# Moving the next sequence's norm and gates to other slots of a gated-delta-rule kernel

## The chip, the cores and the metric

The kernel runs on one core of a Trainium2 chip. The core has five engines that work side by side, each through its own instructions in order: TensorE (PE in the profile; its weight loads are listed apart as PEld), VectorE (DVE), ScalarE (ACT), GpSimd (POOL) and SyncE (SP), which here issues nearly all DMAs. The metric is the device time of one execution in microseconds (us): 2072.44 us is the median of three runs of the kernel before the change, which lie between 2071.39 and 2076.25.

## The reference

The input x holds 4 sequences of 512 tokens with 256 channels, in float32. Cut to what matters:

```python
xn = layernorm(x)                                  # per token
q, k, v, z = split(xn @ W_qkvz.T)                  # 16 q/k heads, 32 v/z heads of 128
b, a       = split(xn @ W_ba.T)                    # two gates per v head
q, k, v = silu(causal depthwise conv of width 4 (q, k, v))
beta = sigmoid(b)
g    = -exp(A_log) * softplus(a + dt_bias)         # log decay per token and head
core = chunked gated delta rule(rmsnorm(q), rmsnorm(k), v, g, beta)
h    = norm_w * rmsnorm(core) * silu(z)
s    = h @ W_out.T
ffn  = (silu(xn @ Wg.T) * (xn @ Wu.T)) @ Wd.T      # weights looked up: lut[idx]
out  = x + s * silu(ffn)
```

The chunked rule inverts, per head and chunk, a unit lower triangular matrix, multiplies values and keys by the inverse, and carries a 128 x 128 state from chunk to chunk. Before any head of a sequence can be worked on, two things of that sequence are needed: its normalised input, transposed to channels by tokens (the tile xnT), and its gates for all 32 heads (the tiles bek, neg, egl, gc and lnb, and the running sums of g as rows in DRAM, g_rows and eg_rows).

## The kernel before, in words

**Items and slots.** The unit of work is an item: one q/k head of one sequence, with its two v heads. There are 64 items, 16 for each of the 4 sequences; item n belongs to sequence n // 16. An item's work is cut into some 115 named steps (`STEPS`), and the string `SLOT` (L973 to L982) writes down one slot: the order of the steps, each with a lag. In slot n the step with lag 5 is done for item n - 5. So about 13 items are in flight, one slot does one item's worth of work on every engine, and the 64 items take 77 slots. The loop at L1024 writes out the program slot by slot; L1061 to L1068 then pin that order on each engine, so no engine takes an instruction ahead of its place.

**Filling.** In the first dozen slots the steps with large lags do not exist yet. The longest path of an item runs through GpSimd: `nt` (DVE, L564), then `nd` and `nl` (two trips through DRAM, DMAs on SP), `L0` to `L3` (GpSimd, 62 small operations, L633 and L639), `yd` and `iu` (two more trips), `tp` (DVE, L660), `m1` and `m2` (small matmuls, L672 to L705), and on to the chunk steps.

**Preparing the next sequence.** `normed(b)` and `gated(b)` (L186 to L287) are generators that compute xnT and the gates of sequence b; `both` (L1010) chains them. They stop at each `yield`, and what lies between two stops is called a step here. For a sequence after the first these are:

- s1 load x (four DMAs on SP); s2 statistics of two of the four token blocks (DVE, L195 and L196); s3 of the other two; s4 the two activations for 1/sqrt (ACT, L88); s5 and s6 subtract and scale, two blocks each (DVE, L204); s7 four transposes (PE, L213) and a copy to xnT (ACT, L215); s8 the same for the other half; s9, for sequences 0 and 1 alone, xnT is also written to DRAM;
- g1 sixteen matmuls (PE, L233) and three DVE operations (L242 to L245); g2 two activations; g3 three DVE operations (L250 to L252); g4 four matmuls (PE, L256), three DVE operations (L265 to L267) and three activations; g5 a DVE operation (L273), eight matmuls (PE, L276) and a DVE copy (L281); g6 g_rows to DRAM; g7 an exponential; g8 eg_rows to DRAM.

**Where these steps go.** `SLOT` holds the mark `Y` twice: at its very start, where the next step is `qm` (called first Y here), and in the middle, behind `x1`, `t10` and `cq2`, where the next step is `yk` (second Y). At each mark a counter `due` grows by one, and `prepare` (L1016), called behind every step, lets the generator go on by one step when `due` is above zero and more than one PSUM bank is free. At slot 8 of a sequence (L1028) the generator of the next one is begun. With two marks a slot, s1 goes to the first Y of slot 8, s2 to the second, s3 to the first Y of slot 9, and so on; for the second sequence, which has s9, g1 falls on the second Y of slot 12, and for the third and fourth, without s9, on the first Y of slot 12 of the sequence before (slots 28 and 44 of the program). Counting the banks that the steps of `SLOT` hold, two or more are free at every one of these places, so no step is put off.

**Fillers.** `X` stands four times in `SLOT` and adds a piece of the weight lookups of the feed-forward part to each slot (L298 to L339, DVE). A job of 16 pieces ends every fourth slot, with a DMA out and a few more operations.

**PSUM banks.** The 8 banks are handed out in turn (`Bank`, L69): who takes a bank waits for the last reader of the tile that had it before.

**The start.** Before the first slot DVE zeroes the four `iut` tiles and the two `tpl` tiles (L120, called from L123 and L124), which hold the inverses; the norm of the first sequence follows.

Of the kernel before, what the change touches and what calls it, by code (L numbers as in the profile page):

```python
# [15 lines left out]
B, S, D = 4, 512, 256  # L16
HQK, HV, HD = 16, 32, 128
# [21 lines left out]
def gated_delta_ffn_kernel(  # L39
# [16 lines left out]
    nc = tc.nc  # L56
# [60 lines left out]

    def zeroed(shape, name):
        t = const.tile(shape, F32, tag=name, name=name)
        nc.vector.memset(t, 0.0)  # L120
        return t

    iut = [zeroed([P, NP, NC, P], f"iut{i}") for i in range(NBUF["iut"])]  # L123
    tpl = [zeroed([P, NP, NC, 2 * Q], f"tpl{i}") for i in range(NBUF["tpl"])]  # L124

    lid = const.tile([R * LH, Q // R, Q], F32, tag="lid", name="lid")
# [856 lines left out]
    plan = [(name, int(lag or 0)) for name, _, lag in (key.partition(":") for key in SLOT.split())]  # L983
# [10 lines left out]
    PASSES.update(dict.fromkeys("tk tq tv0 tv1 th0 th1 ks1 ks2 ks3 pv0 pv1 pv2 pv3 ps0 ps1 ps2 po0".split(), 2))  # L994
    spare, needed = 0, None
    traced = nc.cur_bb.bb.instructions
    begin = traced[-1]
    items, kept, slot = [], [], 0

    def item(n):  # L1000
        return items[n] if 0 <= n < total else None

    def feed():

        nonlocal spare, needed
        while needed is not None and spare >= needed and len(free) > 2:
            spare -= needed
            needed = next(feeding, None)

    def both(b):  # L1010
        yield from normed(b)
        yield from gated(b)

    due = 0

    def prepare():  # L1016

        nonlocal due
        if due and len(free) > 1:
            due -= 1  # L1020
            while next(preparing, None):
                pass

    for n in range(total + last_lag):  # L1024
        if n < total:
            items.append(Item(n))
            b, hq = divmod(n, HQK)
            if hq == HQK // 2 and b + 1 < B:  # L1028
                for _ in preparing:
                    pass  # L1030
                due = 0
                preparing = both(b + 1)
        if n == total + 6:
            for _ in looked:
                pass
            needed = next(feeding)
        slot = n
        for name, lag in plan:
            if name == "X":
                if n >= 6:  # L1040
                    next(looked, None)
            elif name == "Y":
                due += 1
            elif name in MERGES:
                if item(n - lag) or item(n - lag - 1):
                    MERGES[name](item(n - lag), item(n - lag - 1))
            elif item(n - lag):
                STEPS[name](item(n - lag))
                due += n < 4 and name[0] in "ac"
                prepare()  # L1050
            elif needed is not None:
                spare += PASSES.get(name, 0)
                feed()
# [54 lines left out]
```

## Time and profile before

| | us |
|---|---|
| median of 3 runs | 2072.44 (2071.39 to 2076.25) |
| the profiled execution, its own time | 2075.89 |
| its span, first to last instruction | 2073.70 |
| PE busy (matmuls) | 1969.2 (95% of the span) |
| DVE busy | 1775.5 (86%) |
| ACT busy | 1621.0 (78%) |
| POOL busy | 1388.5 (67%) |
| one undisturbed slot (23) from its first `ak` matmul to the next slot's | 27.87 |

All sums are made against one profiled execution; 2.19 us of its time lie around the span. Slots can be read from the trace by the `ak` matmuls (L444): step `ak` has lag 1 and stands shortly ahead of the second Y, so the stretch from the `ak` of slot n to that of slot n + 1 holds what was done at the second Y of slot n (some 3 us after its start) and at the first Y of slot n + 1 (some 15 us after it). Where the engines' busy times stand beside such a stretch, the number in parentheses counts instructions. A time in brackets behind a row of the timeline is how long that engine was idle before the instruction, and who ended the idle time.

### The profile page before, as it was taken

How to read it: one execution, taken by the hardware profiler on the slowest of the kernel's cores; microseconds unless marked ns; L12 is line 12 of the kernel's file. 1: busy time of each engine (PE TensorE's matmuls, PEld its weight loads, DVE VectorE, ACT ScalarE, POOL GpSimd, SP SyncE). 2: the span in 40 equal slices, each digit the busy share in tenths (PEclk: the TensorE clock that was granted, in tenths of full speed). 3: DMA queues.
4: the chain of work that ended last, by engine and by line, in shares of the span. 5: the costliest groups of instructions: out<-in, count | busy, mean ns of one | idle time of the engine just before them, and what ended most of it. 6: DMA issues, size and time to landing. Idle time of an engine off the chain costs nothing.

```text
span 2073.7 us, 48691 instructions
## 1 busy us (share of the span) xinstructions
PE 1969.2 (95%) x15744; PEld 1442.6 (70%) x15744; DVE 1775.5 (86%) x4356; ACT 1621.0 (78%) x4689; POOL 1388.5 (67%) x4181
## 2 busy tenths in 40 slices
PE   6468999999999999999999999999999999998999
PEld 3235777777777777777777777777777777775755
DVE  7788999999999999999998999999999988862323
ACT  5467889888888888888888888888888989963321
POOL 0777777777777767777777767777777777780000
PEclk9779999999999999999999999999999999999999
DMA  2343443344433444334443344443344343321211
GB/s 76 98 107 89 123 106 103 96 108 120 116 103 100 105 111 105 104 100 110 123 108 101 91 119 103 112 105 102 97 113 123 104 108 100 100 75 44 71 51 51
DMA packets 371885, 206.40 MB, mean 100 GB/s; under 512 B 224544, under 2 KB 353712, under 8 KB 371632
## 3 DMA queue, kind: packets, MB, share of 16 engines
q1 hardware_dynamic: 371632, 203.29, 37.3%
q8 instruction: 126, 2.06, 0.4%
q14 instruction: 127, 1.04, 0.2%
HBM read 179.05 MB, written 24.13 MB: 98 GB/s over the span
## 4 chain that ended last, share of the span: by engine, by line
PE 73%; DVE 16%; POOL 3%; ACT 3%; DMA 3%; issue 1%; SPq 1%; DVEq 0%; POOLq 0%; ACTq 0%
PE av L444 9%; PE pp L824 8%; PE pz L478 7%; PE pv L746 5%; PE po L781 4%; PE ak L444 4%; PE pgu L907 4%; PE kk L556 4%; PE po L778 3%; PE aq L444 3%; PE ps L759 3%; PE ks L729 3%; PE th L510 2%; PE pW L703 2%; PE ptv L510 2%; DVE v L456 2%
## 5 line engine op out<-in xcount | busy, mean ns | idle before, releaser
L633 POOL TENSOR_TENSOR pr<-nl,yl 128x60 f32<-128x60 f32 (+24 forms) x1984 | 584.0, 294 | 220.7 <-ACT ik L88 47.6
L639 POOL TENSOR_TENSOR yl<-yl,pr 128x60 f32<-128x60 f32 (+24 forms) x1984 | 605.1, 305 | 155.7 <-DMA yd<-yl 0.4
L456 DVE SCALAR_TENSOR_TENSOR v<-av,cw,v 128x509 f32<-128x509 f32 (+2 forms) x384 | 282.4, 735 | 0.6 <-ACT v L450 0.3
L478 PE MATMUL pz<-xnT,wz 128*128 128x512 f32 x512 | 242.4, 596 | 4.4 <-DVE acc L836 2.5
L824 PE MATMUL pp<-wo,zT 128*128 128x256 f32 x1024 | 243.7, 381 | 0.5 <-DVE zT L816 0.2
L444 PE MATMUL av<-xnT,wv 128*128 128x512 f32 x512 | 241.3, 594 | 1.4 <-DMA wv<-in_w_qkvz 1.4
L824 PEld LDWEIGHTS pp<-wo,zT 128*128 128x128 f32 x1024 | 185.0, 190 | 25.2 <-issue 2.9
L599 POOL TENSOR_TENSOR qe<-qe,q 128x384 f32<-128x384 f32 x128 | 126.3, 1008 | 100.6 <-DMA qe<-eg_rows 52.3
L86 ACT ACT_TABLE_LOAD x128 | 164.2, 1283 | 3.1 <-PEq L1098 0.8
L92 ACT ACT_TABLE_LOAD x128 | 164.2, 1283 | 2.3
L88 ACT ACTIVATE ds<-ds,ls 128x128 f32<-128x128 f32 x512 | 156.9, 390 | 8.2 <-DVE ls L532 6.6
L738 DVE SCALAR_TENSOR_TENSOR r<-ks,neg,vt 128x128 f32<-128x128 f32 x384 | 116.0, 343 | 44.7 <-PE ks L729 42.9
L456 DVE SCALAR_TENSOR_TENSOR q<-aq,cw,q 128x509 f32<-128x509 f32 (+2 forms) x192 | 142.3, 741 | 13.1 <-ACT q L450 10.8
L503 ACT ACTIVATE junk_o<-po 128x128 f32<-128x128 f32 x512 | 142.1, 278 | 14.3 <-PE po L781 2.1
L478 PEld LDWEIGHTS pz<-xnT,wz 128*128 128x128 f32 x512 | 95.5, 190 | 78.8 <-issue 61.2
L456 DVE SCALAR_TENSOR_TENSOR k<-ak,cw,k 128x509 f32<-128x509 f32 (+2 forms) x192 | 141.4, 736 | 2.0 <-ACT k L450 1.6
L746 PEld LDWEIGHTS pv<-r,iut 128*128 128x128 f32 x768 | 105.6, 191 | 46.0 <-issue 38.2
L444 PE MATMUL ak<-xnT,wk 128*128 128x512 f32 x256 | 135.1, 653 | 0.5 <-DMA wk<-in_w_qkvz 0.5
L444 PEld LDWEIGHTS av<-xnT,wv 128*128 128x128 f32 x512 | 87.6, 191 | 65.6 <-issue 63.9
L746 PE MATMUL pv<-r,iut 128*128 128x128 f32 x768 | 124.8, 285 | 8.4 <-DVE r L738 7.5
L444 PE MATMUL aq<-xnT,wq 128*128 128x512 f32 x256 | 120.7, 594 | 2.8 <-DMA wq<-in_w_qkvz 1.8
L495 DVE TENSOR_SCALAR ds<-ds,gc 128x128 f32<-128x128 f32 x512 | 120.9, 305 | 2.0
(177 smaller groups left out, 5058.1 us busy)
## 6 DMA issues: line engine op xcount, KB each, us to landing
ds<-g_rows SPq DMA_DIRECT2D x64, 512.0 KB, 4.0
nl<-nd SPq DMA_DIRECT2D x256, 128.0 KB, 3.9
qe<-eg_rows SPq DMA_DIRECT2D x64, 384.0 KB, 4.3
wv<-in_w_qkvz SPq DMA_DIRECT2D x128, 128.0 KB, 2.4
wz<-in_w_qkvz SPq DMA_DIRECT2D x64, 256.0 KB, 2.8
wo<-in_w_out SPq DMA_DIRECT2D x64, 256.0 KB, 3.1
wk<-in_w_qkvz SPq DMA_DIRECT2D x64, 128.0 KB, 2.5
wq<-in_w_qkvz SPq DMA_DIRECT2D x64, 128.0 KB, 2.3
```

Of the source, the lines that this page charges most:

```text
L86: nc.scalar.preload_act_table_set("natural_log_exp_and_others")
L88: nc.scalar.activation(out, in_, func, **kw)
L92: nc.scalar.activation(out, in_, AF.Silu)
L444: nc.tensor.matmul(ps, lhsT=getattr(it, "w" + x)[:, d, :], rhs=it.xnT[:, d, :], start=(d == 0), stop=(d == DC - 1),)
L456: nc.vector.scalar_tensor_tensor(y[:, sh:], ps[:, : S - sh], cw[:, block(it.hq), j : j + 1], y[:, sh:], ALU.mult, ALU.add)
L478: nc.tensor.matmul(ps, lhsT=it.wz[:, d, p * P : (p + 1) * P], rhs=it.xnT[:, d, :], start=(d == 0), stop=(d == DC - 1),)
L503: nc.scalar.activation(junk, ps[:, c, :], AF.Square, accum_out=out[:, c : c + 1])
L599: nc.gpsimd.tensor_tensor(it.qe[:, p], it.qe[:, p], thirds(it.q, NC)[:, 1:, :], ALU.mult)
L633: nc.gpsimd.tensor_tensor(pr[:, :k, :n], nl[:, j : j + 1, j + 1 :].to_broadcast([R * LH, k, n]), yl[:, :k, j : j + 1].to_broadcast([R * LH ...
L639: nc.gpsimd.tensor_tensor(yl[:, :k, j + 1 :], yl[:, :k, j + 1 :], pr[:, :k, :n], ALU.subtract)
L746: nc.tensor.matmul(pv[:, p, :], lhsT=it.iut[:, p * NC + c, :], rhs=it.r[:, p, :] if c else vt[:, c, :], start=True, stop=True,)
L824: nc.tensor.matmul(ps[:, j, :], lhsT=chunk(hT, 2 * c2 + j), rhs=it.wo[:, p, :], start=(p == 0), stop=(p == NP - 1),)
```

## The change

Three things. The zeroing of `iut` and `tpl` goes from VectorE to GpSimd. The preparation of the next sequence begins at slot 5 (in the first sequence) or slot 4 (in the second and third) in place of slot 8. And the marks do not all count any more: in the first sequence both Y count as before; in later ones only the second Y counts in slots 4 to 10 of the sequence, and both in slots 11 to 15 and 0 to 3.

```diff
     def zeroed(shape, name):
         t = const.tile(shape, F32, tag=name, name=name)
-        nc.vector.memset(t, 0.0)
+        nc.gpsimd.memset(t, 0.0)
         return t
@@
+    last_y = max(i for i, (name, _) in enumerate(plan) if name == "Y")
@@
-            if hq == HQK // 2 and b + 1 < B:
+            if hq == (4 if b else 5) and b + 1 < B:
                 for _ in preparing:
                     pass
                 due = 0
@@
-        for name, lag in plan:
+        for name_at, (name, lag) in enumerate(plan):
             if name == "X":
                 if n >= 6:
                     next(looked, None)
             elif name == "Y":
-                due += 1
+
+                due += n < HQK or n % HQK >= 11 or n % HQK < 4 or name_at == last_y
```

From this follow the places of the steps (1 and 2 are the first and second Y of a slot of the program):

| steps | before | after |
|---|---|---|
| second sequence, s1 to s9 | 8.1, 8.2, 9.1, 9.2, 10.1, 10.2, 11.1, 11.2, 12.1 | 5.1, 5.2, 6.1, 6.2, 7.1, 7.2, 8.1, 8.2, 9.1 |
| second sequence, g1 to g8 | 12.2, 13.1, 13.2, 14.1, 14.2, 15.1, 15.2, 16.1 | 9.2, 10.1, 10.2, 11.1, 11.2, 12.1, 12.2, 13.1 |
| third sequence, s1 to s8 | 24.1, 24.2, 25.1, 25.2, 26.1, 26.2, 27.1, 27.2 | 20.2, 21.2, 22.2, 23.2, 24.2, 25.2, 26.2, 27.1 |
| third sequence, g1 to g8 | 28.1, 28.2, 29.1, 29.2, 30.1, 30.2, 31.1, 31.2 | 27.2, 28.1, 28.2, 29.1, 29.2, 30.1, 30.2, 31.1 |
| fourth sequence | as the third, 16 slots later | as the third, 16 slots later |

## The prediction

> **What bounds the kernel now.** I read the page first: which engine is full.
>
> ```profile
> PE 1969.2 (95%) x15744; PEld 1442.6 (70%) x15744; DVE 1775.5 (86%) x4356; ACT 1621.0 (78%) x4689; POOL 1388.5 (67%) x4181
> ```
>
> PE is, on the mean; what the change is worth must be read where its steps are. So I cut the span at the `ak` matmuls: eight slots without preparation, eight with the third sequence's, eight without, eight with the fourth's.
>
> ```profile
> 346.15:571.37 225.22, 224.40 (x1912) 168.35 (x1905) 217.63 (x535) 198.85 (x577) 174.77 (x519) 1.00 0.42 110
> 571.37:809.11 237.74, 232.84 (x1949) 172.24 (x1941) 227.20 (x558) 201.46 (x587) 175.81 (x523) 1.00 0.40 104
> 809.11:1034.24 225.13, 224.34 (x1911) 168.27 (x1905) 216.32 (x535) 198.81 (x577) 174.51 (x521) 1.00 0.42 109
> 1034.24:1269.81 235.57, 231.84 (x1949) 172.28 (x1941) 223.40 (x558) 201.35 (x587) 171.28 (x519) 1.00 0.40 105
> ```
>
> The reader is to see that a preparation costs 237.74 - 225.22 = 12.5 us for the third sequence and 235.57 - 225.13 = 10.4 us for the fourth, and that without it PE (first number behind the comma) is busy but for 0.8 us: PE bounds these slots. The preparation's own PE work is small: four transposes take 0.44 us of the queue, g1's sixteen matmuls 1.73, g4's four 0.45, g5's eight 1.08, so 2 x 0.44 + 3.26 = 4.1 us. The other 6 to 8 us are waits that the steps bring about. Slot by slot, slot 23 as the yardstick:
>
> ```profile
> 543.50:571.37 27.87, 27.87 (x246) 21.07 (x239) 26.97 (x67) 24.87 (x73) 21.38 (x64) 1.00 0.50 124
> 571.37:600.10 28.73, 28.44 (x247) 21.09 (x239) 28.40 (x74) 24.86 (x73) 23.08 (x70) 1.00 0.38 102
> 600.10:629.38 29.28, 28.76 (x245) 20.88 (x238) 28.08 (x69) 25.14 (x75) 22.42 (x66) 1.00 0.42 113
> 629.38:659.27 29.89, 28.71 (x251) 21.32 (x243) 27.80 (x72) 25.22 (x74) 21.43 (x65) 1.00 0.36 91
> 659.27:691.18 31.91, 31.11 (x267) 23.44 (x259) 28.98 (x73) 25.34 (x74) 22.92 (x69) 1.00 0.40 103
> 691.18:720.78 29.60, 28.92 (x246) 21.13 (x238) 28.79 (x69) 25.25 (x75) 20.76 (x62) 1.00 0.42 104
> 720.78:752.79 32.01, 30.80 (x258) 22.17 (x251) 30.12 (x72) 25.43 (x76) 22.98 (x69) 1.00 0.43 106
> 752.79:781.24 28.45, 28.23 (x247) 21.14 (x239) 28.20 (x71) 25.37 (x74) 20.14 (x61) 1.00 0.39 103
> ```
>
> DVE is nearly as full as PE (26.97 of 27.87). Each stretch holds two steps: s2+s3, s4+s5, s6+s7, s8+g1, g2+g3, g4+g5, g6+g7. The second sequence's g steps lie on the other marks, so that its stretches hold g1+g2, g3+g4, g5+g6:
>
> ```profile
> 227.21:257.72 30.51, 29.73 (x263) 22.88 (x255) 28.30 (x73) 25.63 (x75) 22.87 (x69) 1.00 0.38 95
> 257.72:288.78 31.06, 29.32 (x249) 21.17 (x243) 28.73 (x72) 25.41 (x76) 24.67 (x74) 1.00 0.39 106
> 288.78:318.28 29.50, 29.21 (x254) 21.99 (x246) 28.30 (x74) 24.85 (x73) 19.32 (x58) 1.00 0.39 101
> ```
>
> A lookup job that ends costs 0.91 us in slots 21 and 22 (28.58 and 28.07 against 27.87), and such an end lies in slots 14, 18, 22, 26, 30 and so on. Last, the timeline of PE laid beside slot 23's, instruction by instruction, tells where time is lost:
>
> ```profile
> 634.52 0.24 PE L703 MATMUL pW<-tpl,nt 64*64 64x64 f32 x1 [0.93 <-DVE r L738]
> ...
> 664.82 0.27 PE L705 MATMUL pU<-iut,w 64*64 64x64 f32 x1 [0.66 <-ACT xnT L215]
> ...
> 726.18 0.24 PE L703 MATMUL pW<-tpl,nt 64*64 64x64 f32 x1 [0.76 <-DVE r L738]
> ```
>
> PE waits for a DVE made late by s6 (634.52) and g4 (726.18), and for the bank that s8's copy frees (664.82).
>
> **The change, part by part.** A step's cost is the delay that PE takes on behind it, from that comparison with slot 23.
>
> *Third sequence, s2 to s6, now one a slot at the second Y.* s2 is two L195 of 0.40 and two L196 of 0.18, 1.2 us of DVE. In the stretch from 571.37, s2 at the second Y delays PE by nothing; only when s3 adds 1.2 us is PE late by 0.8. So one such step fits into DVE's slack, two do not: s2, s4, s5 and s6 go to 0. s3 goes to slot 22, where a lookup job ends; s6 stood so in slot 26 and cost 1.0 us (the 0.93 above), 0.2 of it the lookup's. I take 1.0 for s3. Before, s2 to s6 cost 0.86 (28.73 - 27.87) + 0.45 + 0.8 = 2.1; now 1.0.
>
> *s7 and s8.* s7 at the first Y cost 0.85 (0.44 its transposes, 0.41 the wait of `pz` for its bank), s8 at the second 1.4 to 1.6. They change places: no change, 2.3 before and after. With s7 in slot 26, where DVE's lookups end too, it can be 0 to 0.8 more.
>
> *g1 to g8* move half a slot ahead, to the marks that the second sequence has now. There the three stretches cost 2.64 + 3.19 + 1.63 = 7.46, less a lookup's end of 0.91 to 1.13: 6.4. On the old marks the stretches from 659.27 on give 4.04 + 1.73 + 4.14 + 0.58 = 10.5, less 1.6 for s8 and 0.9 for a lookup's end: 8.0. The reason is visible: g3 (1 us of DVE) and g2 cost PE nothing on the new marks, and g5, at the second Y, 1.6. Gain 1.6.
>
> Sum for the third sequence: -(2.1 - 1.0) - 1.6 = -2.7. The fourth is 10.4 / 12.5 of it and its pair g2+g3 cost only 0.83 (28.70 in slot 44) where the third's cost 1.73; I take -1.7.
>
> *Second sequence.* Slots 12 to 14 lose the 6.4 us, which come back elsewhere as far as slots 5 to 11 do not hide them. Those slots fill the pipeline: PE is busy 14.29 of 38.06 us from the `ak` of slot 6, 13.52 of 28.15 in slot 7, 14.68 of 23.14 in slot 8, 26.06 of 34.29 in slot 9. What paces them is the loop through GpSimd:
>
> ```profile
> 53.88 0.24 POOL L633 TENSOR_TENSOR pr<-nl,yl 128x31 f32<-128x31 f32 x1 [47.58 <-ACT ik L88]
> ```
>
> GpSimd waits 47.58 us for the first item's `nt`, which DVE does at 43.88 and two trips through DRAM carry over. s2 at the second Y of slot 5 stands ahead of that `nt` on a DVE that is full there (12.01 of 12.28 us from 36.95): 1.2 us on the path. s3 (6.1) is covered by 4.49 us in which DVE waits for the first lookup indices, s4 to s7 by the 15 us and more in which PE and DVE wait for GpSimd. s8 (8.2) stands between `ak` and `m2` of the item whose inverse is on the path: 0.44 at the clock granted there (0.74 to 0.80), 0.6; a wait for a bank is not due with four free. g1 (9.2) comes before a wait of PE of several us in slot 10: I take 0.3 of its 1.73. g3+g4 and g5+g6 then stand where s6+s7 and s8+s9 stood in slots 10 and 11: 1.8 and 1.6 against 1.8 and 1.5. Sum: -6.4 + 1.2 + 0.6 + 0.3 = -4.3. Ends: -6.4 if all is hidden, +1.2 if nothing is and s2 delays the path too.
>
> *Queues.* s1's four DMA issues (1.80 us at the start, x4) go to slot 5 ahead of the first `ds<-g_rows`, issued at 32.48, 4.0 us to landing; its reader starts at 39.79, so 1.8 us fit; with the transfers in each other's way up to 0.7. In slots 20 and 36 they stand ahead of `nd`, where SP has nothing to issue for 10 us (627.20 to 637.38 in slot 26): 0. g6 and g8 (0.34 each) go to marks that cost nothing in slots 15 and 16. The exponentials of s4, g2, g4 and g7 need the table that `x1` leaves in place for both marks; the 128 loads of each table stay 128. POOL's queue gets nothing but the zeroing.
>
> *Zeroing.* DVE sheds 4 x 0.91 + 2 x 0.49 = 4.6 us, up to 6.2 us, so the statistics (till 8.0) can come earlier. But their reader, `rs` on ACT at 9.00, stands behind this:
>
> ```profile
> 8.86 0.23 ACT L88 ACTIVATE alog<-alog 128x32 f32<-128x32 f32 x1 [6.78 <-DMA alog<-in_a_log]
> ```
>
> The DMA still lands when it lands: gain 0. GpSimd's own rows (0.31 for 256 columns, 0.21 for 128, so 0.95 for 1024 and 0.53 for 512) make 4.9 us; `ones` and `tri` end at 11.2 in place of 6.3, first read at 19.44; `ident`, even if it came behind, at 6.5, needed at 10.08. Cost 0.
>
> *A rule against it.* L204 takes 0.41 us with GpSimd idle (at 9.55) and 0.52 on the mean with GpSimd at work (562 to 800). The Trainium skill (SBUF — State Buffer, Who interferes with whom) says that a VectorE operation in a two-port mode and a GpSimd operation exclude each other for a whole instruction. By that, s5 and s6 in slot 7 would hold up GpSimd, which is on the path there, by 4 x 0.41 = 1.6 us, and the time would be 2065.3 us; the row agrees with some hindrance, and says nothing of who is held up.
>
> **Sum.** -4.3 - 2.7 - 1.7 = -8.7 us: the profiled execution's 2075.89 would be 2067.2. It stands 3.45 above the median of 2072.44, so the forecast is 2072.44 - 8.7 = 2063.7 us.
>
> **Rivals.**
> 1. *The filling hides nothing.* Each moved us comes back in slots 5 to 11, with s2's 1.2 on top: the second sequence gives +1.2 in place of -4.3, and the time is 2069.2. For it: from slot 9 on PE is busy 26 of 34 us. Against: 7 us of waiting in slot 10 alone.
> 2. *The marks make no difference.* The g steps cost the same on either, the second sequence's 6.4 being low because its slots 12 and 13 are not quite full: third and fourth give only the s steps, -1.1 and -0.9, so 2066.1. For it: slot 44's pair was cheap on the old marks too.
> 3. *Slower: the path through GpSimd takes the steps of every slot.* If in slots 5 to 8 each step stands ahead of the `nt` or `tp` on the path (s2 1.2, s3 1.2, s4 0.5, s5 1.0, s6 0.8, s7 and s8 0.44 + 0.6 for the copy each, g1 2.6, `ds` 0.7), that is 10.1 us, against 6.4 saved, and each late DVE piece also pushes the lookups, which wait 2.5 us for their own DMA at 162.81. It decides once the filling loses over 6.4 + 4.4 + 6.2 = 17 us, so 2079 or more. Against: the 4.49 us and 12 to 22 us of idle DVE and PE in these slots.
>
> **How the numbers follow.** 0.3% (6.2 us) is about what a measurement tells from no change. My case, with 2058.5 (-6.4, -4.4 and -3.1 where everything is hidden) to 2066.2: 0.55, and half of rival 2's 0.10 lies there too. Rival 1: 0.20; a mixture of 1 and 2, about 2071: 0.07. Rival 3 or a like one: 0.08. Faster 0.60, same 0.32, slower 0.08. Range 2058.5 to 2072.
>
> **What would show it.** Right: `ak` stretches of slots 12 to 14 at 27.9 to 28.8; slots 20, 21, 23, 24 and 25 without a cost of their own; slots 27 to 30 summing to 6 to 7 us over the yardstick, not 10; `ak` of slot 11, at 199.85, within 3 us of there; `rs` still at 9.0. Wrong: the `ak` of slot 15 (318.28) later than 316; a cost above 1 us in each of slots 21 to 25; more than 128 table loads; PE waiting for `xnT` copies longer than 0.7 us.

## The result and the profile after

| | before, us | after, us | ratio, 95% interval |
|---|---|---|---|
| first comparison | 2072.84 | 2063.70 | 0.9953 [0.9941, 0.9965] |
| second comparison | 2072.97 | 2060.14 | 0.9941 [0.9928, 0.9953] |
| third comparison | 2073.13 | 2062.03 | 0.9947 [0.9934, 0.9959] |

The changed kernel is faster, by 9.1, 12.8 and 11.1 us of the medians. The forecast was 2063.7 us. The profiled execution of the first comparison took 2063.85 us, its span 2062.1.

From the page of the changed kernel, each engine's busy time:

```profile
PE 1966.8 (95%) x15744; PEld 1442.5 (70%) x15744; DVE 1767.1 (86%) x4350; ACT 1620.8 (79%) x4689; POOL 1390.9 (67%) x4187
```

PE is as full as it was, in a shorter span. Six zeroing instructions have gone from DVE (4356 to 4350) to POOL (4181 to 4187). The page counts 128 loads of each table, as before.

The start, ACT in order of time (start, duration, then in brackets the idle time and who ended it):

```profile
5.66 0.30 ACT L88 ACTIVATE rs<-mv,ln_eps 128x4 f32<-128x4 f32 x1 [3.58 <-DVE mv L196]
5.99 0.20 ACT L88 ACTIVATE rs<-rs 128x4 f32<-128x4 f32 x1
8.02 0.23 ACT L88 ACTIVATE alog<-alog 128x32 f32<-128x32 f32 x1 [1.83 <-DMA alog<-in_a_log]
```

Here is the first surprise: `rs` begins at 5.66, not at 9.0, and stands ahead of `alog`. Before, it came straight behind the `alog` of 8.86:

```profile
9.00 0.28 ACT L88 ACTIVATE rs<-mv,ln_eps 128x4 f32<-128x4 f32 x1
```

The `ak` of slot 4 begins at 29.18 in place of 31.36.

The second sequence: three `ak` stretches, of slots 12, 13 and 14 (length; then PE, PEld, DVE, ACT and POOL busy; the granted clock, the DMA share, GB/s):

```profile
226.54:254.83 28.29, 28.26 (x247) 21.18 (x239) 28.08 (x69) 25.27 (x74) 23.12 (x71) 1.00 0.41 105
254.83:283.28 28.45, 28.34 (x246) 20.90 (x239) 27.36 (x67) 24.84 (x73) 23.14 (x69) 1.00 0.45 117
283.28:311.37 28.09, 27.93 (x245) 21.03 (x238) 27.53 (x72) 24.83 (x73) 21.59 (x64) 1.00 0.39 97
```

They were 30.51, 31.06 and 29.50: 6.24 us have gone, and PE now waits for next to nothing there.

The third sequence, stretches of slots 22 and 25 to 30 of the changed kernel:

```profile
508.65:537.80 29.15, 27.93 (x246) 21.03 (x238) 28.34 (x75) 24.83 (x73) 21.71 (x65) 1.00 0.39 100
...
593.54:622.09 28.55, 28.34 (x247) 20.89 (x239) 27.78 (x68) 24.82 (x73) 22.54 (x67) 1.00 0.45 116
622.09:652.37 30.28, 29.65 (x254) 21.92 (x246) 27.24 (x69) 25.67 (x75) 22.92 (x68) 1.00 0.37 90
652.37:683.52 31.15, 30.21 (x262) 22.93 (x254) 28.68 (x72) 25.55 (x75) 21.27 (x66) 1.00 0.41 107
683.52:713.40 29.88, 28.88 (x250) 21.37 (x242) 28.05 (x71) 25.40 (x76) 22.49 (x68) 1.00 0.41 100
713.40:743.58 30.18, 29.70 (x254) 21.82 (x246) 28.26 (x70) 24.83 (x73) 20.63 (x62) 1.00 0.45 119
743.58:771.67 28.09, 27.94 (x246) 21.04 (x238) 27.37 (x71) 25.34 (x74) 21.75 (x65) 1.00 0.41 100
```

The stretches of slots 20, 23 and 24, not shown, are 27.87 each: the undisturbed slot's length with s1, s4 and s5 in them. Slot 22, with s3 and a lookup's end, takes 29.15 where the lookup's end alone took 28.07. In its 29.15 us PE is busy 27.93, and this row of PE's timeline says where 1.22 us went:

```profile
514.07 0.24 PE L703 MATMUL pW<-tpl,nt 64*64 64x64 f32 x1 [1.22 <-DVE r L738]
```

It is the wait for a late DVE that s6 caused in slot 26 before (0.93).

**Where the time went.** All kernels of this study were cut at the same `ak` matmuls, so that several executions stand behind each number. A kernel is counted as old or new in a row of the table by what it does in those slots; one that does neither is left out of that row.

| stretch, us | old there: mean (lowest to highest) | new there: mean (lowest to highest) | difference | forecast |
|---|---|---|---|---|
| start to `ak` of slot 4 | 30.8 (30.2 to 31.4), 5 kernels | 28.5 (28.0 to 29.2), 7 | -2.2 | 0 |
| slots 4 to 11 | 195.8 (194.9 to 196.7), 6 | 196.8 (195.8 to 197.6), 7 | +1.0 | +2.1 |
| slots 12 to 14 | 91.4 (91.1 to 91.9), 6 | 84.8 (84.5 to 85.2), 8 | -6.7 | -6.4 |
| slots 16 to 31, third sequence | 462.1 (461.3 to 463.0), 5 | 460.2 (459.6 to 460.8), 5 | -1.9 | -2.7 |
| slots 32 to 47, fourth sequence | 460.7 (459.9 to 461.2), 5 | 459.6 (458.9 to 460.3), 5 | -1.1 | -1.7 |

The sum is -10.9 against a forecast of -8.7. The two first profiles alone would have flattered the forecast: from them the second, third and fourth sequences give -4.7, -2.7 and -1.4. But the profile of before lies at the top of its group in the third sequence (462.96, in a group from 461.3) and near the bottom of it in slots 4 to 15 (314.79, in a group from 314.65 to 315.85). Within a group such a stretch differs by up to 1.8 us from one execution to another.

### The profile page after: what moved, and what is told of

Read it like the earlier page. It is cut to its first block, busy times and chain, and to the rows that moved or that the text cites. A ratio compares the mean times of both kernels' runs of the same rounds, so it can differ in the third digit from the quotient of the medians.

```text
span 2062.1 us, 48693 instructions
## 1 busy us (share of the span) xinstructions
PE 1966.8 (95%) x15744; PEld 1442.5 (70%) x15744; DVE 1767.1 (86%) x4350; ACT 1620.8 (79%) x4689; POOL 1390.9 (67%) x4187
## 4 chain that ended last, share of the span: by engine, by line
PE 74%; DVE 17%; POOL 3%; DMA 2%; ACT 2%; issue 1%; SPq 1%; DVEq 0%; POOLq 0%; ACTq 0%
PE av L444 9%; PE pp L824 8%; PE pz L478 7%; PE pv L746 5%; PE po L781 4%; PE ak L444 4%; PE aq L444 4%; PE pgu L907 4%; PE kk L556 4%; PE po L778 3%; PE ps L759 3%; PE ks L729 3%; PE th L510 2%; PE pW L703 2%; DVE v L456 2%; PE ptv L510 2%
## 5 line engine op out<-in xcount | busy, mean ns | idle before, releaser
L633 POOL TENSOR_TENSOR pr<-nl,yl 128x60 f32<-128x60 f32 (+24 forms) x1984 | 588.5, 297 | 213.4 <-DMA nl<-nd 47.1
L639 POOL TENSOR_TENSOR yl<-yl,pr 128x60 f32<-128x60 f32 (+24 forms) x1984 | 599.5, 302 | 155.6 <-DMA yd<-yl 0.2
```

Of the source, the lines that this page charges most:

```text
L633: nc.gpsimd.tensor_tensor(pr[:, :k, :n], nl[:, j : j + 1, j + 1 :].to_broadcast([R * LH, k, n]), yl[:, :k, j : j + 1].to_broadcast([R * LH ...
L639: nc.gpsimd.tensor_tensor(yl[:, :k, j + 1 :], yl[:, :k, j + 1 :], pr[:, :k, :n], ALU.subtract)
```

## Experiments

### The zeroing alone

```diff
 # the kernel before
-        nc.vector.memset(t, 0.0)
+        nc.gpsimd.memset(t, 0.0)
```

> The kernel before with the zeroing of iut and tpl on GpSimd, nothing else. Theory: on ACT the two rs activations now stand ahead of alog's exponential, so the first norm ends earlier and all behind it follows; the ak of slot 4 comes at 29.2 us in place of 31.36, and the 2.2 us are still there at slot 16 (343.9 in place of 346.15) and in the time (-2.2 us). Rival: the loop through GpSimd sets the pace of the filling anyway and swallows the head start; ak of slot 4 at 29.2 but slot 16 at 346, the time unchanged. Rival of the prediction: no gain even at slot 4 (31.4).

Measured 2070.52 us, ratio 0.9991 [0.9982, 1.0000]. ACT's timeline at its start:

```profile
5.25 0.30 ACT L88 ACTIVATE rs<-mv,ln_eps 128x4 f32<-128x4 f32 x1 [3.17 <-DVE mv L196]
5.58 0.20 ACT L88 ACTIVATE rs<-rs 128x4 f32<-128x4 f32 x1
7.96 0.23 ACT L88 ACTIVATE alog<-alog 128x32 f32<-128x32 f32 x1 [2.18 <-DMA alog<-in_a_log]
```

DVE is done with the statistics at 5.15, `rs` follows at once, and `alog` waits for its DMA behind it. The `ak` of slot 4 comes 3.18 us earlier than in the profile of before, that of slot 16 2.72: in these two executions most of the head start is still there when the pipeline is full. The time falls by 1.8 us, at the edge of what the comparison resolves. The order of `alog` and `rs` is nowhere in the edit. The kernel pins the order of its slots only (L1061 to L1068); ahead of the first slot, the build chooses it, and it chose another once the zeroing had left DVE.

### The order alone, both ways

The first kernel has the zeroing on GpSimd and holds `rs` behind `alog`; the second has the zeroing on VectorE and holds `alog` behind `rs`. Both edits are cut to what matters.

```diff
 # the kernel before, with the zeroing on GpSimd
+        ln = exp_ln(rs, mv[:, :, 1], AF.Ln, bias=ln_eps)
+        if b == 0:
+            tc.add_manual_dep(ln.ins, first.ins.name, ...)
...
+    first = exp_ln(alog, alog, AF.Exp)
```

```diff
 # the kernel before
+        ends[b] = exp_ln(rs, rs, AF.Exp, scale=-0.5)
...
+    tc.add_manual_dep(exp_ln(alog, alog, AF.Exp).ins, ends[0].ins.name, ...)
```

> The kernel before with the zeroing on GpSimd, as in the first experiment, but with the exponential of alog pinned ahead of the rs activations on ACT, as the kernel before has them. Theory (the gain of the zeroing is that ACT's order changes, so that rs no longer waits for the DMA of alog): rs at 8.0 to 9.0, behind alog, the ak of slot 4 at 30.2 to 31.4 as in the runs with the old order, and the time of the kernel before (0, at most -0.5 us). Rival (the freed VectorE time counts by itself): -1.8 us as in the first experiment.

> The kernel before, zeroing on VectorE, with the exponential of alog pinned behind the rs activations on ACT. Theory (the start has two waits one behind the other, VectorE's zeroing up to 6.2 us and the DMA of alog up to 7.9 or 8.9): rs at 8.1, when the statistics are done; the ak of slot 4 at 30.2 to 30.6, so 0 to 0.9 us less than before, and the time about -0.4 us. Rival (ACT's order is the whole gain): rs at 5.7, -1.8 us as with the zeroing on GpSimd.

Measured 2072.82 us, ratio 1.0000 [0.9991, 1.0009], and 2073.08 us, ratio 1.0001 [0.9992, 1.0011]. ACT in the kernel with the zeroing on GpSimd and `alog` first:

```profile
7.90 0.23 ACT L88 ACTIVATE alog<-alog 128x32 f32<-128x32 f32 x1 [5.82 <-DMA alog<-in_a_log]
8.03 0.28 ACT L88 ACTIVATE rs<-mv,ln_eps 128x4 f32<-128x4 f32 x1
```

ACT in the kernel with the zeroing on VectorE and `alog` last:

```profile
8.09 0.30 ACT L88 ACTIVATE rs<-mv,ln_eps 128x4 f32<-128x4 f32 x1 [6.01 <-DVE mv L196]
8.42 0.20 ACT L88 ACTIVATE rs<-rs 128x4 f32<-128x4 f32 x1
8.54 0.21 ACT L88 ACTIVATE alog<-alog 128x32 f32<-128x32 f32 x1
```

Two things hold `rs` at about 8 us: the DMA that `alog` ahead of it waits for, and a DVE that zeroes before it does the statistics. The times by themselves can't tell 1.8 us from nothing here, as the intervals overlap with that of the zeroing alone; the rows of the start do. With either of the two left, the gain is gone: the `ak` of slot 4 begins at 31.09 and 30.14, against 28.0 to 29.2 without both. So the zeroing's gain needs both, a DVE that is free early and an `rs` that does not stand behind `alog`; neither brings it by itself.

### The moves alone, and the second sequence alone

The first kernel is the changed one with the zeroing left on VectorE; the second has only this edit.

```diff
 # the kernel before; both marks count everywhere
-            if hq == HQK // 2 and b + 1 < B:
+            if hq == (8 if b else 5) and b + 1 < B:
```

> The changed kernel with the zeroing back on VectorE. Theory, parts add up: slot 4 at 31.4, slot 16 4.3 to 4.7 us earlier than before (341.5 to 341.9), slots 16 to 32 2.7 shorter, 32 to 48 1.4 shorter, in all -8.5 to -9. Rival: the second sequence's early steps fit into slots 5 to 9 only because of the head start; then slot 16 is less than 3 us earlier and the time falls by 7 or less.

> The kernel before, with only the second sequence's preparation begun at slot 5; third and fourth sequence as before. Theory (the filling hides most of it): slot 16 4.3 us earlier (341.8), nothing after it, -4.3 us. Rival 1 of the prediction (the filling hides nothing): slot 16 about 1 us later (347.3), +1.2 us.

Measured 2063.11 us, ratio 0.9957 [0.9945, 0.9970], and 2067.16 us, ratio 0.9978 [0.9969, 0.9987]: -9.2 and -5.2 us. The early steps of the second sequence thus fit without the head start of the zeroing too. The second sequence alone, slots 4 to 11, 12 to 14, and 4 to 15:

```profile
31.10:227.59 196.49, 138.22 (x1025) 90.17 (x1023) 162.34 (x392) 132.89 (x375) 135.67 (x413) 0.84 0.41 104
227.59:312.08 84.49, 84.25 (x722) 63.06 (x714) 82.34 (x206) 74.92 (x218) 67.01 (x201) 1.00 0.43 107
31.10:339.95 308.85, 250.34 (x1978) 174.30 (x1976) 271.56 (x662) 232.66 (x664) 225.01 (x680) 0.90 0.41 105
```

In the second stretch PE is busy but for 0.24 us: of the preparation only g7 and g8 are left there, and they cost PE nothing. In the first, which is as long as in the old kernels (194.9 to 196.7), PE does 28 matmuls more and DVE 11 operations more than before in nearly the same time. That is rival 1 refuted: the filling hides most of what is moved into it.

### The changed kernel again

It was run unchanged beside the later experiments, twice.

> The changed kernel once more, beside the next three on one chip: 2063.7 us as measured, ratio 0.995 to 0.997; its trace is the yardstick for the two variants of it.

> The changed kernel a third time, as the yardstick of this set: by the sum of the first experiment (-1.8 us) and the second (-9.2 us) 11 us less than the kernel before, ratio 0.9947.

Measured 2060.14 us, ratio 0.9941 [0.9928, 0.9953], and 2062.03 us, ratio 0.9947 [0.9934, 0.9959]. Together with the first comparison's 2063.70, the changed kernel's medians differ by 3.6 us, those of the kernel before by 0.3. So differences of 1 to 2 us between variants of the changed kernel are read below from the stretches of the trace, and not from the times.

### s2 off the path

The second sequence's s2 goes from the second Y of slot 5 to the first Y of slot 6.

```diff
 # the changed kernel, at the mark
+                if n in (5, 6):
+                    due += (name_at == 0) * (n == 6) - (name_at == last_y) * (n == 5)
```

> The changed kernel with the second sequence's s2 moved from the second Y of slot 5, where it stands ahead of the first nt, to the start of slot 6, where VectorE waits for the first lookup indices; s3 follows it there, the rest as in the changed kernel. Theory: the first GpSimd operation of the items comes 1.2 us earlier and slot 12 and all behind it too, -1.2 us against the changed kernel. Rival (the filling is paced elsewhere): the first GpSimd operation earlier, but slot 12 and the time unchanged.

Measured 2061.56 us, ratio 0.9947 [0.9934, 0.9959]; the changed kernel beside it had 2060.14. First, DVE in the changed kernel, where s2 stands ahead of the first `nt`:

```profile
40.96 0.42 DVE L195 BATCH_NORM_STATS2 st<-xs 128x6 f32<-128x256 f32 x1
...
41.94 0.18 DVE L196 BATCH_NORM_AGGREGATE mv<-st 128x2 f32<-128x6 f32 x1
42.04 0.99 DVE L546 TENSOR_TENSOR kd<-ptk,kb 128x384 f32<-128x384 f32 x2
42.95 1.41 DVE L564 TENSOR_TENSOR nt<-kk,ds 128x256 f32<-128x256 f32 x4
```

Then POOL's first operation on the first item, in the changed kernel run beside the experiment:

```profile
51.62 0.24 POOL L633 TENSOR_TENSOR pr<-nl,yl 128x31 f32<-128x31 f32 x1 [40.82 <-DMA nl<-nd]
```

and in the experiment, where `kd` comes straight behind the operation that s2 followed:

```profile
50.62 0.24 POOL L633 TENSOR_TENSOR pr<-nl,yl 128x31 f32<-128x31 f32 x1 [39.82 <-DMA nl<-nd]
```

GpSimd begins 1.0 us earlier, though the `ak` of slot 4 came 0.6 us later here (28.98, against 28.37 in the changed kernel beside it). Counted from that `ak`, the first `nt` starts at 13.64 to 13.79 us in the seven executions with s2 ahead of it, at 12.52 to 12.73 in the six old ones, and at 12.65 in this experiment: s2 delays it by 1.1 us. How much of that reaches GpSimd differs. From the start of `nt`, through two trips through DRAM, to GpSimd's first operation it took 8.65 to 10.00 us. In the changed kernel's three executions GpSimd began 23.25 to 23.41 us behind the `ak` of slot 4, in this experiment 21.64, in the old kernels 21.65 to 22.52. But with s2 ahead and the zeroing on VectorE (the moves alone, the second sequence alone) it began at 22.31 and 22.29, as in the old ones. In the two variants of the last experiment below it was 22.86 and 22.60. Here is the row of the second sequence alone, whose `ak` of slot 4 is at 31.10:

```profile
53.39 0.24 POOL L633 TENSOR_TENSOR pr<-nl,yl 128x31 f32<-128x31 f32 x1 [47.10 <-ACT lk L88]
```

The last of the four `nl` transfers landed there at 53.23, so that GpSimd waited for it, although the row names ACT. Why the trips differ stays open.

With s2 out of the way, slots 4 to 15 took 307.6 us in place of 308.9 to 310.1, and slots 4 to 11 took 194.9, no longer than in the old kernels. The time itself was not lower, though; between the two kernels' own scatters, 1 to 2 us can't be told. It is shown that s2 holds up `nt`. That the filling is shorter without it rests on one execution, and that moving it makes the kernel faster is not shown.

### The pacing alone

The third and fourth sequences begin at slot 4 and take one step a slot, but up to slot 11, so that the g steps keep their old marks. The second sequence and the zeroing are as before.

```diff
 # the kernel before
-            if hq == HQK // 2 and b + 1 < B:
+            if hq == (4 if b else 8) and b + 1 < B:
...
-                due += 1
+                due += n < HQK or n % HQK >= 12 or n % HQK < 4 or name_at == last_y
```

> The kernel before, with the third and fourth sequence begun at slot 4 at one step a slot (second Y) up to slot 11, and two from slot 12, so that g1 to g8 stay on the marks that the kernel before has; second sequence and zeroing as before. Theory (pacing is worth little, since s3 meets a lookup's end and s7 goes to the dearer mark): third and fourth sequence -0.5 us each, -1 us in all; what the changed kernel gains beyond that in them comes from the marks of s8 and g1 to g8. Rival 2 of the prediction (the marks are worth nothing, the pacing is all): third -2.7, fourth -1.4, -4 us in all.

Measured 2069.97 us, ratio 0.9986 [0.9977, 0.9994]: -3.2 us of the medians. Its third and fourth sequences:

```profile
346.63:807.54 460.91, 455.88 (x3853) 340.87 (x3845) 443.04 (x1092) 400.00 (x1163) 349.70 (x1040) 1.00 0.41 108
807.54:1267.21 459.67, 454.82 (x3853) 340.86 (x3845) 437.19 (x1092) 399.94 (x1163) 344.45 (x1039) 1.00 0.41 107
```

Against the old kernels' means that is -1.2 and -1.0, so 2.2 of the 3.0 us that the whole change gains in these two sequences. What is left for the marks of the g steps is 0.7 and 0.1 us, as far as one execution can tell: the third sequence lies 0.35 us below the lowest of the old kernels, the fourth 0.25.

### The marks alone

The g steps on the new marks with the old pacing: the first Y of slots 24 and 40 does not count, and every step behind it comes half a slot later.

```diff
 # the kernel before
-                due += 1
+                due += not (n >= HQK and n % HQK == 8 and name_at == 0)
```

> The kernel before, but in slots 24 and 40 the first Y does not count, so that every step of the third and fourth sequence falls half a slot later, on the other mark; still two a slot, from slot 8. Theory (the marks matter for g1 to g8, 1.6 us in the third and about 0.9 in the fourth; s2 to s6 still stand in pairs, s7 and s8 change places): slots 24 to 33 1.6 us shorter in the third, 0.9 in the fourth, -2.5 us in all. Rival 2 of the prediction (the g steps cost the same on either mark): 0.

Measured 2072.00 us, ratio 0.9997 [0.9988, 1.0006]; the third sequence 461.5 us, the fourth 460.1: 0.6 us below the old kernels' mean in each. The half slot's delay puts g5 and g6 into the stretch of slot 30, where a lookup job ends:

```profile
749.28:778.85 29.57, 29.28 (x253) 21.96 (x247) 28.59 (x74) 24.80 (x73) 18.66 (x57) 1.00 0.37 93
```

That stretch took 28.45 before, but with g6 and g7 in it. In the second sequence of the kernel before, the same pair stood beside a lookup's end, too, in slot 14, and took 29.50. So the g steps have here the marks and the neighbours from which the forecast took its 6.4 us. Their stretches, slots 28 to 30, sum to 91.64 us: 8.0 over the yardstick, 7.1 less a lookup's end. The edit moves s2 to s8 by half a slot as well, so it does not size the marks of the g steps by themselves. By this run the marks are worth 1.1 us in both sequences together, by what the pacing run leaves 0.8, each from one execution; both are well under the 2.4 us forecast.

### s3 away from the lookup's end

The third and fourth sequences begin a slot earlier, and nothing is done in the slot with the lookup's end. The first kernel also puts s7 on the first Y of slot 10 of the sequence; the second leaves s7 and all behind it where the changed kernel has them.

```diff
 # the changed kernel
-            if hq == (4 if b else 5) and b + 1 < B:
+            if hq == (3 if b else 5) and b + 1 < B:
...
-                due += n < HQK or n % HQK >= 11 or n % HQK < 4 or name_at == last_y
+                h = n % HQK
+                if n < HQK or h >= 11 or h < 3:
+                    due += 1
+                elif h == 10:                # in the first kernel only
+                    due += name_at == 0      # in the first kernel only
+                elif h != 6:
+                    due += name_at == last_y
```

> The changed kernel with the third and fourth sequence's steps kept off the two slots in which a lookup job ends: begun at slot 3, s1 to s3 at the second Y of slots 3, 4, 5, nothing in slot 6, s4 to s6 in 7, 8, 9, s7 at the first Y of slot 10, s8 and all g steps where the changed kernel has them. Theory (s3 costs 1.0 us and s7 0.6 more because they meet the lookups' extra VectorE work): slots 22 and 38 back to 28.1 to 28.2, 1.6 us less in each of the two sequences, -3 us against the changed kernel (2060.5). Rival (a step costs PE this much wherever it is): no change against it, 2063.7.

Measured 2060.92 us, ratio 0.9944 [0.9930, 0.9957]. Its stretches of slots 22, 25 and 26:

```profile
507.94:536.02 28.08, 27.94 (x246) 21.07 (x239) 27.39 (x71) 24.81 (x73) 21.18 (x64) 1.00 0.41 104
...
591.88:621.99 30.11, 29.11 (x250) 21.17 (x243) 28.13 (x68) 25.18 (x74) 23.57 (x71) 1.00 0.41 109
621.99:651.40 29.41, 29.00 (x251) 21.36 (x243) 27.88 (x71) 25.17 (x74) 21.04 (x63) 1.00 0.38 94
```

Slot 22 is back at the 28.07 that the lookup's end costs by itself: s3's 1.07 us was the collision. But s7 on the mark right behind s6 makes slot 25 1.56 us longer, and slot 26 gains only 0.87, so 0.7 of what was saved is spent there. The time is 0.8 us above that of the changed kernel beside it, where 3 us less were expected. The second kernel:

> The changed kernel with the third and fourth sequence begun at slot 3 and no step in slot 6 alone: s1 to s3 at the second Y of slots 3 to 5, s4 to s7 of slots 7 to 10, the rest where the changed kernel has it. Theory (s3 meets the lookup's end in slots 22 and 38, and s7 is better at the second Y of slot 10 than at the first): slots 22 and 38 at 28.1, the stretches of slots 25, 26, 41 and 42 as in the changed kernel, 1.0 us less in each sequence, -2.1 us against the changed kernel. Rival (what s3 gives up is paid in another slot): stretches of slots 21 and 37 longer by as much, no gain.

Measured 2060.25 us, ratio 0.9941 [0.9929, 0.9954]; the changed kernel beside it had 2062.03 us, 0.9947 [0.9934, 0.9959]. Its third and fourth sequences:

```profile
337.98:797.34 459.36, 455.41 (x3851) 340.68 (x3844) 440.36 (x1092) 400.23 (x1163) 350.03 (x1039) 1.00 0.41 108
797.34:1255.54 458.20, 454.31 (x3853) 340.49 (x3845) 435.31 (x1092) 400.15 (x1163) 345.82 (x1041) 1.00 0.40 107
```

and the changed kernel's, from the run beside it:

```profile
336.89:796.95 460.06, 455.12 (x3853) 340.59 (x3845) 440.96 (x1092) 400.22 (x1163) 348.25 (x1039) 1.00 0.41 108
796.95:1255.85 458.90, 453.95 (x3853) 340.47 (x3845) 435.56 (x1094) 400.11 (x1163) 345.60 (x1042) 1.00 0.41 107
```

Both are 0.7 us shorter, the lowest seen of any kernel, and slots 22 and 38 are back at 28.06 and 28.12. In the third sequence 0.5 of that is paid again in slot 20, which has s2 now and takes 28.41; in the fourth it is not (27.95 in slot 36). The time is 1.8 us lower than that of the changed kernel beside it, but another of the changed kernel's medians, 2060.14, is as low. So a gain of some 0.7 us in each sequence is what these stretches suggest, and no time settles it.

## Why the prediction was right, and where it was wrong

**The total** was forecast at -8.7 us and came out between -9.1 and -12.8. The mechanism, preparation steps moved to where DVE or PE has slack, is what the stretches show. Of the terms, one was missing, and three were off in size. That the first comparison's median is the forecast's 2063.7 to the tenth is luck: the zeroing and the second sequence gave 3.6 us more than forecast, the third and fourth 1.4 less, and the same kernel's two other medians are 2060.14 and 2062.03.

**Zeroing: forecast 0, measured -2.2 us at slot 4 and -1.8 us in the time of the zeroing alone.** The step that failed is the sentence that the reader of the statistics, `rs`, "stands behind" `alog` and that "the DMA still lands when it lands". The DMA did land as late, at about 8 us; but `rs` no longer stood behind it. The forecast took an order read from the trace of before for a fixed one, at the one place where the kernel does not pin it. The two kernels that hold the order show that the gain needs both, the free DVE and `rs` ahead. Of the rest of this term, GpSimd's own rows were right: 0.95 us for 1024 columns and 0.53 for 512, as worked out, and `tri`, ready at 10.8, held up nobody. `ident` was ready at 2.3, ahead of most of the zeroing. But "Cost 0" left something out. The zeroing pushes GpSimd's L131 back from 1.60 to 6.25, where it runs beside the four L204 of the first norm. First the kernel before, then the changed one:

```profile
9.55 1.38 DVE L204 TENSOR_SCALAR xs<-xs,mv,rs 128x256 f32<-128x256 f32 x4 [1.55 <-ACT rs L88]
6.23 2.10 DVE L204 TENSOR_SCALAR xs<-xs,mv,rs 128x256 f32<-128x256 f32 x4 [0.67 <-ACT rs L88]
```

From `rs` to the first `ak` it is 6.92 to 6.94 us in the six kernels with the zeroing on VectorE, and 7.54 to 7.84 in the eight with it on GpSimd. So the -2.2 us are what is left after a cost of 0.6 to 0.9.

**Second sequence: forecast -4.3, measured -5.7.** Slots 12 to 14 gave what was forecast, 6.7 against 6.4. The filling took back 1.0 us, not 2.1. s2's 1.2 us ahead of the first `nt` was right as a delay of `nt` (1.1 us); at GpSimd's first operation it is seen in some executions and not in others. With s2 moved away, and s8, g1, s5 and s6 where the changed kernel has them, slots 4 to 11 took 194.9 us, as in the old kernels (194.9 to 196.7). So in that execution the 0.6 for s8 and the 0.3 for g1, taken from rows where PE has no slack, can't be found. The trace gives no sign of the 1.6 us by the Trainium skill's rule (SBUF — State Buffer, Who interferes with whom) either: those 194.9 us have no room for it, and no run shows that L204 works in a two-port mode. The rule holds in the rows this far, that L204 and GpSimd's operations do lengthen each other somewhat (below).

**Third and fourth: forecast -2.7 and -1.7, measured -1.9 and -1.1.** s3 in slot 22 at 1.0 us was right (29.15 - 28.07 = 1.1), and so were s1, s2, s4 and s5 at nothing (slots 20, 23 and 24 at 27.87; slot 21 at 28.58, which a lookup's end costs alone). s6 was not at nothing: slot 25 shows 0.7. s7 and s8, with a lookup's end in slot 26, cost 30.28 - 27.87 - 0.91 = 1.5 and not 2.3, which makes up for it. The pacing, forecast at -1.1 and -0.9, gave -1.2 and -1.0. The term that was mis-sized is the marks, -1.6 and -0.8: they are worth 0.7 and 0.1. The forecast took the new marks' cost from the second sequence's stretches and the old marks' from the third's, in one execution that stood 0.9 us above the mean of its group. With the changed kernel's own rows, slots 27 to 30 sum to 119.30 - 4 x 27.87 = 7.8 us over the yardstick, where the forecast named 6 to 7; less 0.9 for a lookup's end that is 6.9, not 6.4, and the marks run has 7.1. The old marks' four stretches are 9.4 to 10.5 over the yardstick in the five old kernels, 9.8 on the mean: less 1.6 for s8 and 0.9 for a lookup's end, 7.3 and not 8.0. So the new marks were dearer than forecast, and the old ones were not as dear.

**Rivals.** Rival 1, that the filling hides nothing (+1.2), is refuted by the second sequence alone: -5.2 us. Rival 2, that the marks make no difference, is closer to the truth than the forecast's 2.4 us, though its price (2066.1) was not reached, since the zeroing and the filling gave more. Rival 3 needed 17 us in the filling; it took 1.0.

**Still open.** Whether skipping only the slot of the lookup's end is a gain over the changed kernel (1.8 us by the medians), and why 1.0 us off the path ahead of GpSimd, which the stretches of one execution show, does not show in the time.

## What to carry to other kernels

An order read from a trace is a fact only where the kernel pins it; where the build chooses, ask what an edit to one engine may reorder on another, and price that as an unknown. Work that does not fit beside a full engine can be hidden in a pipeline's filling, one step at a time; look there for the operation that feeds the pacing loop, since a step of 1.2 us put ahead of it made it 1.1 us late here. And price a step of 1 us from several executions: here one stretch of 460 us scatters by 1 to 2 us.

## What the runs showed of the hardware

- The small DMA of `alog` let its reader begin anywhere from 7.89 to 8.86 us in thirteen profiled executions, seven of them by 7.96. In the old order the start moves with it: of the five kernels with the zeroing on VectorE and `alog` ahead of `rs`, the three with `alog` at 7.9 have the `ak` of slot 4 at 30.2 to 30.8, the two with 8.31 and 8.86 at 31.1 and 31.4. The kernel with the old order and the zeroing on GpSimd is at 31.1 with `alog` at 7.90: its four L204 took 1.88 us beside GpSimd, not 1.38.
- Four L204 operations on 256 columns took 2.10 us together at 6.23 of the changed kernel, with GpSimd's L131 running from 6.25 on, and 1.38 us at 9.55 of the kernel before, with GpSimd idle. In slots 7 and 8 of the changed kernel, at 68.62 and 88.60, beside GpSimd's L633 and L639, two took 0.84 and 0.73 us (two with GpSimd idle: 0.73). GpSimd's L633 that began at 596.16, in the midst of two L204, took 0.42 us, against 0.30 on the mean of all its 1984; the eight L131 took 3.94 us with L204 beside them and without.
- The undisturbed slot repeats to the hundredth (27.87 in slots 20, 23 and 24 of the changed kernel's first profile and in slot 23 of the one before), while 16 slots with a preparation in them scatter by 1 to 2 us from one execution to the next.
- The four transfers of the first item's `nl` took 3.9 to 5.1 us from the first issue to the last landing (3.93 in the second sequence alone, 5.13 in the kernel before).
